# One decoder kernel, last attention: row sums from added pairs of exponential tiles, and the queries' copy on another engine

## The chip, the cores and the metric

The kernel runs on one core of a Trainium2 chip. A core has several engines with a queue of instructions each: TensorE (PE) for matmuls, VectorE (DVE) and ScalarE (ACT) for element-wise work, GpSimd (POOL), and SyncE (SP), which issues transfers here. Matmuls write to PSUM, and the other engines move results from there to SBUF. The metric is device microseconds of one execution.

## What is computed

A decoder of four blocks, each with self-attention, cross-attention to a context, and a feed-forward part. The change is in the last cross-attention. Batch 4, 256 queries of width 128, a context of 1601 rows of width 96, 16 heads of width 64:

```python
def _L3_xattn_ref(x, context, Wq, Wk, Wv, Wo, bo):
    HEADS, DIM_HEAD = 16, 64
    b, n, _ = x.shape
    h, d = (HEADS, DIM_HEAD)
    scale = d ** (-0.5)
    q = (x @ Wq).reshape(b, n, h, d).transpose(0, 2, 1, 3)
    k = (context @ Wk).reshape(b, -1, h, d).transpose(0, 2, 1, 3)
    v = (context @ Wv).reshape(b, -1, h, d).transpose(0, 2, 1, 3)
    sim = jnp.einsum('bhid,bhjd->bhij', q, k) * scale
    attn = jax.nn.softmax(sim, axis=-1)
    out = jnp.einsum('bhij,bhjd->bhid', attn, v)
    out = out.transpose(0, 2, 1, 3).reshape(b, n, h * d)
    return out @ Wo + bo
```

The softmax needs, for each query, the maximum of the scores over 1601 keys, the exponentials, their sum (the row sum, which the output is divided by), and their product with the values.

## The kernel before

The network runs in stages. `l3_xattn` is the last. It goes through 32 units: a batch and a pair of heads (`hp`) each. A unit has four steps of up to four chunks of 128 keys. Scores are held transposed, keys on the partitions: `scores(g)` makes a tile `St` of 128 x 1024 for two chunks (two heads x two chunks x 256 queries). Steps 0 to 2 have two such tiles (k = 0 to 5), step 3 has one of 65 rows (k = 6). Everything is float32.

The pieces of a unit, with the names by which the trace shows them:

- `queries` (L1894): projection of the queries by TensorE, copied from PSUM to the tile `Q` (L1900). `projections` (L1902): keys of one step and values of another, copied by ScalarE to `K` and `V` (L1931).
- `scores` (L1933): `big<-Q,K` on TensorE, copied by ScalarE to `St` (L1943).
- `running` (L1945): VectorE keeps the element-wise maximum of the unit's tiles in `kept[:, :4]` (shown as `w`; L1950 for the first two, L1953 for the others) and folds the two chunks (L1957).
- `maxima` (L1959): TensorE transposes the folded maxima (`one<-c,mx`), VectorE reduces (L1969). `spread` (L1971): TensorE brings the maxima back to all key rows (`one<-c,mq`), ScalarE copies them to `Mb` (L1981).
- `shifted` (L1983): VectorE subtracts `Mb` from each `St` in place (L1987). `weights` (L1991): ScalarE takes exponentials in place (L1994).
- `sums` (L1996): TensorE multiplies values and exponentials (`one<-St,V`), and then the exponentials by 32 columns of ones (`one<-St,c`), four products a tile: head h and chunk c go to their own strip of 32 partitions in the upper half of the accumulator `acc`. A float32 product is two records in the trace.
- `ended` (L2029): when a unit's sums are complete, ScalarE copies the strips to `rows` (L2026), TensorE adds them over chunks with the matrix `both`, VectorE takes the reciprocal (L2035) and multiplies (L2038). After a batch's eighth unit there follow the output projection (`one<-w,w`), the residual and normalisation (L535, L486 to L497) and, in `l3_ffn`, the quantised last layer (L2091 to L2122).

The order on TensorE, VectorE and ScalarE is written out by hand in the loop at L2061; each engine works its queue strictly in that order. Iteration `g` works on step `g` of the scores and, five steps later (`gb = g - LAG`), on the exponentials; the sums come one iteration after that. So in the iteration with `g % 4 == 0` stand the last running maximum of one unit, the shift of step 3 and the sums of step 2 of the unit before, and the maxima; in the next one the spread and the shift of step 0.

Small PSUM tiles (`misc`, shown as `one`) have two buffers; `acc`, the queries' projection, the maxima and the spread share them.

The stage starts while two chains of the stage before (batches 2 and 3 of the fourth self-attention layer, `life` at L1739 with `late` true) are still unfinished. They are carried over and advanced once an iteration (`later`). Their tiles `h`, `x1`, `x3` and `xn` lie in parts of the tile `kept`, which `places` hands out (L1885): `h` is `kept[:, 4:8]`.

Of the kernel before, what the change touches and what calls it, by code (L numbers as in the profile page):

```python
# [21 lines left out]
B, T, D = 4, 256, 128  # L22
# [281 lines left out]
class Net:  # L304
# [1416 lines left out]
    def l3_attn(self):  # L1721
        nc = self.nc
        slots = []
        for g in range(4):
            t = self.tile(f"QK{g}", [P, 2, T], bufs=1)
# [13 lines left out]
        def life(b):  # L1739
            if b == B - 1:  # L1740
                yield from self.taken_over()[0]
            start = x = self.x[b]
            for i in range(NL):
                pk = f"p3_{i}"
                late = i == NL - 1 and b >= B - 2
                if not late:
                    xb = self.tile("xb", wide, bufs=4)
                    nc.gpsimd.tensor_add(xb, x, row(pk, "bo"))
                if i or b not in self.ahead:
                    self.ahead[b] = yield from self.normed_T(  # L1750
                        x, self.w(pk, "ln1_w"), self.w(pk, "ln1_b")
                    )
                xT = self.ahead[b]
                values[b] = self.self_values(b, self.w(pk, "Wv"), self.w(pk, "bv"), xT, 8)
                ps = self.misc()
                self.mm(ps[:, :T], self.w(pk, "Wq"), xT)
                self.mm(ps[:, T:], self.w(pk, "Wk"), xT)
                qk = self.tile("qk", [P, 2, T], bufs=4)
                nc.scalar.activation(qk[:, 0, :], ps[:, :T], AF.Identity, bias=self.w(pk, "bq"))
                nc.vector.tensor_scalar_add(qk[:, 1, :], ps[:, T:], self.w(pk, "bk"))  # L1760
                outs[b] = self.tile("heads", wide, bufs=4, pool=self.act)
                ready[b], left[b] = (i, qk), 4
                yield
                while left[b]:
                    yield
                yield CUT if late else None
                if late:
                    xb = self.tile("xb", wide, bufs=1)
                    nc.gpsimd.tensor_add(xb, x, row(pk, "bo"))
                oT = self.transposed(  # L1770
                    outs[b], "oT", bufs=1 if late else 2, engine=nc.scalar
                )
                yield
                ps = self.misc()
                for n in range(NB):
                    self.mm(
                        ps[:, n * D : (n + 1) * D], oT[:, n * P : (n + 1) * P], self.w(pk, "Wo")
                    )
                x1 = self.late("x1") if late else self.tile("x1", wide, bufs=4)
                nc.vector.tensor_add(x1.rearrange(flat), ps[:, : NB * D], xb.rearrange(flat))  # L1780
                xb = self.tile("xb", wide, bufs=1 if late else 4)
                nc.gpsimd.tensor_add(xb, x1, row(pk, "b2"))
                xT = yield from self.normed_T(
                    x1, self.w(pk, "ln2_w"), self.w(pk, "ln2_b"), self.late("xn") if late else None
                )
                h = self.late("h") if late else self.tile("h", [P, 4, T])
                banks = {}
                for k in range(4):
                    if k % 2 == 0:
                        banks[k // 2] = self.misc()  # L1790
                    at = banks[k // 2][:, k % 2 * T : (k % 2 + 1) * T]
                    self.mm(at, self.w(pk, "W1")[:, k * P : (k + 1) * P], xT)
                    if k == 1 and not late:
                        continue
                    for j in ((k - 1, k) if late else range(4)) if k % 2 else ():
                        nc.scalar.activation(
                            h[:, j, :], banks[j // 2][:, j % 2 * T : (j % 2 + 1) * T], AF.Gelu,
                            bias=self.w(pk, "b1")[:, j : j + 1],
                        )
                yield  # L1800
                yield
                ps = self.misc()
                w2 = self.w(pk, "W2").rearrange("p (c d) -> p c d", c=4)
                for n in range(NB):
                    to = ps[:, n * D : (n + 1) * D]
                    for c in range(4):
                        self.mm(
                            to, h[:, c, n * P : (n + 1) * P], w2[:, c, :],
                            start=c == 0, stop=c == 3,
                        )  # L1810
                if late:
                    x = self.late("x3")
                elif i == NL - 2 and b >= B - 2:
                    x = self.y()
                else:
                    x = self.tile("x3", wide, bufs=4)
                nc.vector.tensor_add(x.rearrange(flat), ps[:, : NB * D], xb.rearrange(flat))
                finished[i] += 1
                if i == 0 and finished[0] == B:
                    self.load("p5")  # L1820
            z = yield from self.normed_steps(
                x, "xn", bufs=2, out=self.late("xn") if b >= B - 2 else None
            )
            nc.gpsimd.tensor_mul(z, z, row("p5", "fw"))
            nc.gpsimd.tensor_add(z, z, row("p5", "fb"))
            yield
            y = self.y()
            nc.vector.tensor_add(y, z, start)
            yield from self.block_end_steps(b, y)
# [35 lines left out]
    def l3_xattn(self):  # L1865
# [5 lines left out]
        nc = self.nc  # L1871
# [4 lines left out]
        steps = 4 * len(units)  # L1876
        qs, ks, vs, sts, mx, top, accs, outs = {}, {}, {}, {}, {}, {}, {}, {}
# [4 lines left out]
        nc.gpsimd.tensor_copy(wb, w8.bitcast(I8))  # L1882
        kept = self.tile(f"w{SLOT['p3_1']}", [P, 11, T], pool=self.wpool)
        one = [kept[:, i].rearrange("p (n d) -> p n d", n=NB) for i in range(8, 11)]
        places = {"h": kept[:, 4:8], "x1": one[0], "x3": one[1], "xn": one[2]}  # L1885
        self.late = places.get

        def parts(g):
# [5 lines left out]
        def queries(u):  # L1894
            b, hp = units[u]
            ps = self.misc()
            for d in halves:
                self.mm(ps[d, :T], wq[:, hp * P + d.start : hp * P + d.stop], self.xT[b])
            qs[u] = self.tile("Q", [P, T], bufs=2)
            nc.vector.tensor_copy(qs[u], ps[:, :T])  # L1900

        def projections(gk, gv):  # L1902

# [87 lines left out]
        def weights(g):  # L1991
            for k, nc_, kp in parts(g):
                e = sts[g // 4, k][:kp, :, :nc_, :]
                nc.scalar.activation(e, e, AF.Exp, scale=HD**-0.5)  # L1994

        def sums(g):  # L1996
            u = g // 4
            if g % 4 == 0:
                accs[u] = self.misc()
            acc = accs[u]  # L2000
            es = [(k, nc_, sts.pop((u, k))[:kp]) for k, nc_, kp in parts(g)]
            for k, nc_, e in es:
                for c in range(nc_):
                    i = 2 * k + c
                    for h, d in enumerate(halves):
                        if i < NCH - 1:
                            self.mm(
                                acc[d, :T], vs[g][:, i - g % 4 * 4, d], e[:, h, c, :],
                                start=i == 0, stop=False,
                            )  # L2010
            for k, nc_, e in es:
                kp = e.shape[0]
                for c in range(nc_):
                    for h in range(2):
                        d = slice(HD * h + SW * c, HD * h + SW * c + SW)
                        self.mm(
                            acc[d, T:], self.w("c", "ones", kp)[:, :SW], e[:, h, c, :],
                            start=False, stop=False,
                        )
                if kp < P:  # L2020
                    for h, d in enumerate(halves):
                        self.mm(acc[d, :T], vs[g][:kp, 0, d], e[:, h, 0, :], start=False)
            vs.pop(g)
            if g % 4 == 3:
                rows = self.tile("rows", [P, T], bufs=1)
                nc.scalar.copy(rows, acc[:, T:])  # L2026
                later.append(ended(u, rows))
# [32 lines left out]
        with self.tc.manual_schedule(engines=engines):  # L2060
            for g in range(-1, steps + LAG + 2):  # L2061
                gb = g - LAG
                if g % 4 < 2 and 0 <= g - 1 < steps:
                    running(g - 1)
                if g % 4 == 1 and 4 < g <= steps + 1:
                    spread(g // 4 - 1)
                if 0 <= gb < steps:
                    shifted(gb)
                if 0 <= g + 1 < steps and (g + 1) % 4 == 0:
# [11 lines left out]
                    running(g - 1)  # L2081
                if 0 <= g < steps:
                    scores(g)
            while later:
                self.advance(later)

# [58 lines left out]
```

## Time and profile before

| | us |
|---|---|
| three runs | 2769.0, 2773.4, 2780.3 (median 2773.41) |
| profiled execution, its own time | 2769.6 |
| its span, first to last instruction | 2767.8 |
| mean granted TensorE clock | 0.98 |
| last attention, from its first projection of queries | 1896.7 to the end |

Busy time from 1896.7 us to the end (871.1 us): TensorE 847.2, VectorE 610.5, ScalarE 552.3, GpSimd 23.3. Durations of single instructions in the stage (mean, taken from 2100 to 2750 us by shape):

| line, what | ns |
|---|---|
| L1987 shift, VectorE, 128x1024 | 1218 |
| L1953 running maximum, VectorE, 128x1024 | 1220 |
| L1950 first maximum, VectorE, 128x1024 | 1225 |
| L2035 reciprocal, VectorE, 128x256 | 1757 |
| L1900 queries' copy, VectorE, 128x256 | 416 |
| L1994 exponentials, ScalarE, 128x1024 | 1079 |
| L1943 score copy, ScalarE, 128x1024 | 1023 |
| L2026 copy of strips, ScalarE, 128x256 | 373 |

How to read it: a line of the timeline gives the start in us from the beginning of the span, the length, the engine, the line of the kernel, the operation with output<-input, the shape (partitions x elements), a count where like instructions follow each other, and in brackets the idle time before it with what ended that. Lengths of neighbours may overlap a little, since an engine begins an instruction before the one ahead has fully ended; the distance from start to start is what a queue needs. Several matmuls on different strips of the array run at once, so the mean of one record times the count is more than the time they take.

### The profile page before, as it was taken

What the parts mean: (1) busy time and instruction counts of PE and PEld (TensorE: products, weight loads), DVE (VectorE), ACT (ScalarE), POOL (GpSimd) and SP (SyncE); (2) the same over time, 40 slices, a digit from 0 to 9 for tenths busy, and PEclk for the clock granted to TensorE, in tenths of its full rate; (3) what the DMA queues carried; (4) which work ended last, traced back from release to release, by engine and by line L of the source; (5) the groups of instructions that cost most, each with busy time, mean ns of one, the idle gap of its engine ahead of it and who ended that gap; (6) DMA issues with size and microseconds to landing.
All of it is one profiled execution on the core that took longest, in us unless ns stands there. A gap on an engine that the chain in (4) does not pass through costs nothing.

```text
span 2767.8 us, 63295 instructions
## 1 busy us (share of the span) xinstructions
PE 2620.8 (95%) x26619; PEld 1708.1 (62%) x26619; DVE 1747.2 (63%) x3802; ACT 1526.2 (55%) x2931; POOL 180.2 (7%) x199
## 2 busy tenths in 40 slices
PE   6999999988879999999899999999999999999997
PEld 4555555555555555555797777776566666666665
DVE  5666666465457665655355666666677677677675
ACT  2455555635534555555554555556666576576573
POOL 2000100120020000000001011111000000000000
PEclk8999999989999999999999999999999999999999
DMA  3000000000120000000002010000000000000000
GB/s 111 2 1 1 2 1 1 1 21 15 27 88 17 2 1 1 1 2 1 1 1 87 20 25 13 13 12 3 1 1 2 4 2 1 3 2 2 3 2 3
DMA packets 14684, 34.57 MB, mean 12 GB/s; under 512 B 4025, under 2 KB 7229, under 8 KB 13505
## 3 DMA queue, kind: packets, MB, share of 16 engines
q1 hardware_dynamic: 14400, 30.53, 4.0%
q8 instruction: 210, 3.44, 0.5%
q14 instruction: 74, 0.60, 0.1%
HBM read 23.67 MB, written 0.52 MB: 9 GB/s over the span
## 4 chain that ended last, share of the span: by engine, by line
PE 88%; DVE 6%; ACT 3%; issue 2%; POOL 1%; DMA 0%; POOLq 0%; ACTq 0%; DVEq 0%
PE one L399 63%; PE big L399 13%; PE acc L399 8%; DVE M L909 1%; PE one L835 1%; PE one L544 1%; PE one L472 1%; DVE St L1987 1%; PE one L1324 1%; DVE mpad L697 1%; ACT E L731 0%; DVE w L1953 0%; DVE rec L2035 0%; POOL rn L1257 0%; ACT w L1314 0%
## 5 line engine op out<-in xcount | busy, mean ns | idle before, releaser
L909 DVE TENSOR_REDUCE M<-one 128x1 f32<-128x458 f32 (+3 forms) x1024 | 528.2, 567 | 290.8 <-PE one L399 289.8
L932 ACT ACTIVATE E<-one 128x512 f32<-128x512 f32 (+1 forms) x896 | 457.7, 563 | 420.8 <-PE one L399 420.7
L399 PE MATMUL one<-Q,K 32*128 32x256 f32 (+1 forms) x3328 | 531.8, 402 | 1.5 <-DVE M L909 1.5
L399 PE MATMUL one<-K,Q 32*128 32x458 f32 (+3 forms) x2048 | 459.2, 541 | 1.6 <-DVE M L909 1.6
L399 PEld LDWEIGHTS one<-Q,K 32*128 32x128 f32 (+1 forms) x3328 | 310.6, 180 | 62.3 <-DVE M L909 35.5
L1943 ACT COPY St<-big 128x1024 f32<-128x1024 f32 (+1 forms) x224 | 204.3, 959 | 160.0 <-PE big L399 160.0
L399 PEld LDWEIGHTS one<-K,Q 32*128 32x128 f32 x2048 | 171.2, 185 | 143.8 <-issue 79.3
L1987 DVE TENSOR_TENSOR St<-St,Mb 128x1024 f32<-128x1024 f32 (+1 forms) x224 | 245.2, 1141 | 1.8 <-ACT Mb L1981 1.8
L399 PE MATMUL acc<-E,V 128*32 128x256 f32 (+1 forms) x3328 | 233.2, 387 | 7.1 <-ACT E L932 7.1
L1994 ACT ACTIVATE St<-St 128x1024 f32<-128x1024 f32 (+1 forms) x224 | 215.1, 1014 | 25.4 <-DVE St L1987 25.3
L731 ACT ACTIVATE E<-one 128x384 f32<-128x384 f32 (+1 forms) x352 | 154.3, 525 | 115.0 <-PE one L399 114.8
L399 PE MATMUL big<-Q,K 64*128 64x256 f32 (+1 forms) x1664 | 214.4, 393 | 0.0
L399 PE MATMUL one<-St,V 128*64 128x256 f32 (+1 forms) x1664 | 205.7, 384 | 0.4
L492 POOL TENSOR_TENSOR ln_r<-ln_ve,half 128x2 f32<-128x2 f32 x92 | 71.0, 772 | 2070.0 <-DVE ln_ve L490 2015.8
L1953 DVE TENSOR_TENSOR w<-w,St 128x1024 f32<-128x1024 f32 (+1 forms) x160 | 178.5, 1116 | 34.8 <-ACT St L1943 27.6
L399 PE MATMUL one<-xT,w 128*128 128x256 f32 (+1 forms) x664 | 170.9, 398 | 18.8 <-DVE Q L1127 8.3
L692 DVE TENSOR_REDUCE Ms<-one 128x3 f32<-128x384 f32 x256 | 130.1, 550 | 89.0 <-PE one L399 87.8
L399 PEld LDWEIGHTS big<-Q,K 64*128 64x128 f32 (+1 forms) x1664 | 147.7, 183 | 57.5 <-issue 40.2
L399 PEld LDWEIGHTS acc<-E,V 128*32 128x32 f32 (+1 forms) x3328 | 87.3, 109 | 125.0 <-issue 70.0
L399 PEld LDWEIGHTS one<-St,V 128*64 128x64 f32 (+1 forms) x1664 | 114.3, 137 | 63.4 <-issue 15.9
L399 PEld LDWEIGHTS big<-w,ctx 96*64 96x64 f32 x1664 | 96.8, 137 | 54.0 <-issue 53.9
L399 PEld LDWEIGHTS one<-xT,w 128*128 128x128 f32 (+1 forms) x664 | 97.1, 181 | 50.2 <-issue 15.6
(308 smaller groups left out, 3743.7 us busy)
## 6 DMA issues: line engine op xcount, KB each, us to landing
QK<-qk SPq DMA_DIRECT2D x256, 16.0 KB
w<-in_p SPq DMA_DIRECT2D x12, 274.0 KB
rows<-in_ctx_rows SPq DMA_DIRECT2D x4, 630.5 KB
ctx<-in_ctx SPq DMA_DIRECT2D x4, 600.4 KB
w<-in_down SPq DMA_DIRECT2D x1, 2112.0 KB
w<-in_up SPq DMA_DIRECT2D x1, 1632.0 KB
w<-in_gp SPq DMA_DIRECT2D x1, 1632.0 KB
w<-in_p SPq DMA_DIRECT2D x4, 384.0 KB
```

Source lines behind the costliest of these rows:

```text
L399: self.nc.tensor.matmul(out, lhsT, rhs, start=start, stop=stop)
L472: self.nc.tensor.transpose(ps[:, n * P : (n + 1) * P], x[:, n, :], self.ident)
L492: nc.gpsimd.tensor_tensor(rstd, ve, self.half[:, :NB], ALU.pow)
L544: self.nc.tensor.transpose(ps[:rows, n * P : (n + 1) * P], m4[:, n, :rows], self.ident)
L692: nc.vector.reduce_max(out=m[:, j, :], in_=ps[:, : 3 * P].rearrange("p (s c) -> p s c", c=P), axis=AX.X,)
L731: nc.scalar.activation(es[t, j], ps[:, :w], AF.Exp, scale=scale)
L909: nc.vector.reduce_max(out=ms[i][:, n, j, part : part + 1], in_=ps[:, at : at + hi - lo], axis=AX.X)
L932: nc.scalar.activation(e[:kp, :w], ps[:kp, :w], AF.Exp, scale=scale)
L1943: nc.scalar.copy(st[:kp, :, :nc_, :], ps[:kp, :, :nc_, :])
L1953: nc.vector.tensor_max(to, to, sts[u, k][:kp, :, :nc_, :])
L1987: nc.vector.tensor_sub(e, e, top[u][:kp].unsqueeze(2).broadcast_to([kp, 2, nc_, T]))
L1994: nc.scalar.activation(e, e, AF.Exp, scale=HD**-0.5)
```

## The change

Three things are changed in the last attention.

1. A new function `added(g)` has VectorE add the two tiles of exponentials of a step into `kept[:, 4:8]`. It is called for step 2 of a unit in the iteration after its exponentials, behind `running` and ahead of `shifted`, and for step 0 at the end of the iteration that makes its exponentials. `sums` then multiplies only the sum by the ones: 4 products instead of 8.
2. A flag `busy` guards the buffer. The late chains wait for it and hold it from their entry until `x3` is made; `added` does nothing while it is held, and then the step's row sums are taken as before.
3. The queries' copy goes from VectorE to ScalarE.

```diff
@@ life(b)
                 yield CUT if late else None
+                while late and self.late("busy")[0]:
+                    yield
                 if late:
+                    self.late("busy")[0] = True
                     xb = self.tile("xb", wide, bufs=1)
...
                 nc.vector.tensor_add(x.rearrange(flat), ps[:, : NB * D], xb.rearrange(flat))
+                if late:
+                    self.late("busy")[0] = False
@@ l3_xattn
-        places = {"h": kept[:, 4:8], "x1": one[0], "x3": one[1], "xn": one[2]}
+        busy, pairs = [False], {}
+        places = {"busy": busy, "h": kept[:, 4:8], "x1": one[0], "x3": one[1], "xn": one[2]}
@@ queries(u)
-            nc.vector.tensor_copy(qs[u], ps[:, :T])
+            nc.scalar.copy(qs[u], ps[:, :T])
@@
+        def added(g):
+
+            if not busy[0]:
+                u, k = g // 4, g % 4 * 2
+                busy[0] = True
+                pairs[g] = kept[:, 4:8].rearrange("p (h c) t -> p h c t", h=2)
+                nc.vector.tensor_add(pairs[g], sts[u, k], sts[u, k + 1])
@@ sums(g)
-            for k, nc_, e in es:
+            if g in pairs:
+                busy[0] = False
+            for k, nc_, e in [(0, 2, pairs.pop(g))] if g in pairs else es:
                 kp = e.shape[0]
@@ loop over g
                 if g % 4 == 1 and 4 < g <= steps + 1:
                     spread(g // 4 - 1)
+                if gb % 4 == 3 and 0 < gb <= steps:
+                    added(gb - 1)
                 if 0 <= gb < steps:
                     shifted(gb)
...
                 if 0 <= g < steps:
                     scores(g)
+                if gb % 4 == 0 and 0 <= gb < steps:
+                    added(gb)
```

## The prediction

> **What bounds the kernel now.** The page first: TensorE (PE) is busy for 95% of the span and makes up 88% of the chain that ended last.
>
> ```profile
> PE 2620.8 (95%) x26619; PEld 1708.1 (62%) x26619; DVE 1747.2 (63%) x3802; ACT 1526.2 (55%) x2931; POOL 180.2 (7%) x199
> ...
> PE 88%; DVE 6%; ACT 3%; issue 2%; POOL 1%; DMA 0%; POOLq 0%; ACTq 0%; DVEq 0%
> ```
>
> A busy PE is not a PE at its peak, so I go to the stage. The last attention runs from about 1897 us to the end: 32 units (a pair of heads of one batch), each of four steps, of which 19 follow each other at 24.59 us (from one row of L1969 to the next). The busy time of the engines in one such unit (columns: window, length, busy PE, PEld, DVE, ACT, POOL, granted clock, DMA share, GB/s):
>
> ```profile
> 2211.99:2236.58 24.59, 24.59 (x268) 15.43 (x264) 17.93 (x18) 16.86 (x24) 0.00 (x0) 1.00 0.01 1
> ```
>
> PE has no gap; VectorE (DVE) is idle for 6.66 us. Last the timeline of that unit, which shows what waits for what (start, length, engine, line, output<-input, count, idle time before it):
>
> ```profile
> 2210.99 1.07 PE L399 MATMUL one<-St,c 128*32 128x256 f32 x16
> 2212.00 1.09 PE L399 MATMUL one<-c,mx 128*64 128x128 f32 x16
> ...
> 2217.36 4.62 DVE L1987 TENSOR_TENSOR St<-St,Mb 128x1024 f32<-128x1024 f32 x4
> 2217.70 0.62 PE L399 MATMUL one<-St,c 65*32 65x256 f32 x4
> ...
> 2218.26 0.65 PE L399 MATMUL one<-St,V 65*64 65x256 f32 x4
> 2218.36 0.59 ACT L1931 COPY V<-big 128x512 f32<-128x512 f32 x1
> 2218.84 2.02 ACT L1994 ACTIVATE St<-St 128x1024 f32<-128x1024 f32 x2
> ...
> 2222.53 1.76 DVE L2035 RECIPROCAL rec<-one 128x256 f32<-128x256 f32 x1 [0.55 <-PE one L399]
> ...
> 2224.66 2.54 DVE L1953 TENSOR_TENSOR w<-w,St 128x1024 f32<-128x1024 f32 x2
> ```
>
> ```profile
> 2229.73 2.54 DVE L1953 TENSOR_TENSOR w<-w,St 128x1024 f32<-128x1024 f32 x2
> ...
> 2232.05 0.65 PE L399 MATMUL big<-Q,K 64*65 64x256 f32 x4
> ...
> 2233.41 0.69 DVE L1953 TENSOR_TENSOR w<-w,St 65x512 f32<-65x512 f32 x1 [1.14 <-ACT St L1943]
> ...
> 2234.14 0.69 DVE L1957 TENSOR_TENSOR mx<-w 128x512 f32<-128x512 f32 x1
> ...
> 2234.75 0.68 DVE L1987 TENSOR_TENSOR St<-St,Mb 65x512 f32<-65x512 f32 x1
> ...
> 2235.58 1.07 PE L399 MATMUL one<-St,c 128*32 128x256 f32 x16
> ```
>
> Call T0 the start of the ones-matmuls of step 2 (2210.99, next 2235.58). The reader is to see two places: the four shifts of 2217.36 run without a gap although the exponentials of the first two end only at 2220.86; and between the small scores (2232.05) and T0 VectorE has only running maximum, fold and one small shift.
>
> **The change part by part.**
>
> *PE, removed.* Step 0 and step 2 keep 8 of 16 records of one<-St,c. Sixteen take 1.00 us from start to start (2206.46 to 2207.46; here to 2212.00); a group of 4 records, which on two column strips runs in two turns as 8 will on four, takes 0.56 (2217.70 to 2218.26). So an add removes 0.44 us, 0.88 in a full unit. The flag leaves the additions out while the late chains of batches 2 and 3 hold the buffer: unit 0 has one, units 2 and 3 none, all others two, 59 in all. 59 x 0.44 = 26 us if nothing else moved.
>
> *VectorE, added.* An add is a tensor_tensor of 128x1024 like L1950: 1.22 us, 1.14 to the next independent instruction (2216.22 to 2217.36 there). Its place on the queue decides.
>
> Add of step 0: it stands between the shifts of steps 0 and 1 and waits for both exponentials of step 0. These end at T0 + 9.87 now (2220.86), and T0 + 9.43 with the shorter ones-matmuls. The shifts of step 0 are over at about T0 + 8.2, so VectorE stands still for 1.2 us, and all that is queued behind waits with it: shifts of step 1, reciprocal, product, maxima of step 1, shifts and maxima of step 2, maximum of step 3, fold, and the second add.
>
> Add of step 2: it stands behind the fold, ahead of the small shift, and the ones-matmuls of step 2 wait for it. From the start of the small scores PE comes to them 3.53 us later (2232.05 to 2235.58); the fold lets an add start after 2.70 (2234.75), so it ends at 3.92 and PE can start at 3.97, with the 0.05 that PE takes after VectorE (the maxima's reduce ends at 2724.97, PE starts at 2725.02). Even with VectorE on time PE waits 0.44, as much as this add saves it.
>
> The loop from T0 to T0, all from rows of this unit: first add starts T0 + 9.46 (0.03 after ScalarE, as at L1953: copy ends 2233.38, maximum 2233.41); + 1.14 add; + 2.27 two shifts (2227.12 to 2229.39); + 1.79 reciprocal; + 0.34 product; + 2.46 maxima of step 1 (2224.66 to 2227.12); + 2.27 shifts of step 2; + 2.64 maxima of step 2 (each is followed by one that needs its result, 1.32 as in the row of three at 2182.44); + 0.73 and 0.61 maximum of step 3 and fold; + 1.22 second add; + 0.05 = 24.98. That is 0.39 more than 24.59: **VectorE's queue with the wait in it becomes the bound**, and PE, which would need 23.71, idles about 1.27 a unit, most of it ahead of the ones-matmuls of step 2.
>
> *Queries' copy.* 0.42 (0.34 to the next) leaves VectorE; the loop above has it out already. ScalarE takes 0.37 for such a copy (L2026). It comes behind the score copies of step 2, where ScalarE idled 1.20 before K<-big, so it is hidden; without that cover it would cost 0.37 at most. In a batch's last unit PE waited 0.48 for the copy by VectorE; that goes. The queries' matmul needs the buffer which the product frees, at T0 + 15.1 in the new order, and PE is there at T0 + 15.1: nothing lost.
>
> *Units beside the regular 19.* (a) Three times a batch ends. In the unit with the output projection (2145.34 to 2154.33) VectorE idles 9.15 us and catches up, so PE decides: - 0.88 - 0.48 + 0.44 = -0.9. In the next one VectorE has 2.37 us of output chain behind the first add (2172.36 to 2174.73), 0.51 further on (2181.93 to 2182.44), and the quantisation before the maxima's reduce, which makes PE's spread 0.31 later: 24.98 + 2.37 + 0.51 + 0.31 = 28.2 against 25.67 (2160.74 to 2186.41), +2.5. Together +1.6, three times +4.8. (b) Units 0 to 4: -0.44 up to unit 3, then unit 4, with 1.27 (as at 1924.58 to 1925.85) + 0.51 of late layernorm in the loop and no shortened ones-matmul at its start (+ 0.44): 27.2 against 25.11, +2.1; together +1.7. (c) The last interval has little PE work (22.44); the loop makes it 25.0, +2.5; in the tail behind it some 0.9 is gained.
>
> Sum: 19 x 0.39 = 7.4, + 4.8 + 1.7 + 2.5 - 0.9 = **+15.5 us**.
>
> **Two rules against the rows.** The Trainium skill (Perfetto Trace Analysis, Identifying the Most-Contended Engine) calls occupancy a fair measure for VectorE and says to work on the engine with most of it. VectorE would have 17.93 - 0.41 + 2.44 = 19.96 us in a unit, 84% of PE's 23.71; by that rule PE stays the bound and all 26 us are won. The timeline says +15.5, since VectorE's 1.2 us of waiting and the 9.46 before the first add are in the loop. I take the timeline.
>
> The second concerns the new PE waits. The skill (TensorE: Matmul & The Clock Gate, What's actually happening) has the clock halve after an idle window of about 3.4 us; waits of 1.3 would be free. This trace halves it sooner: after 1.54 us of idling, with 0.80 a little before, the granted clock is 0.50 (columns as above):
>
> ```profile
> 2729.00:2730.00 1.00, 0.00 (x1) 0.00 (x0) 1.00 (x2) 0.92 (x2) 0.00 (x0) 1.00 0.00 0
> ...
> 2732.00:2733.00 1.00, 1.00 (x8) 0.63 (x6) 1.00 (x1) 0.88 (x1) 0.00 (x0) 0.50 0.00 0
> ```
>
> There sixteen matmuls with V took 3.46 instead of 1.90 us. But single waits of 1.03 to 1.10 us amid dense matmuls (thirteen between 82 and 1229 us) left it at 1.00, and so did 1.25 at 1523; only one of 1.16 at 616.7, in a stretch with other gaps, was followed by 0.51. Sparse stretches are not this stage, so the forecast has no halving; its price by the row of 3.46 would be 1.6 us each time.
>
> **The rivals.**
>
> 1. *The additions are hidden.* If VectorE's idle 6.66 us took them in and PE stayed the bound: -26 us, **2744**. For it: occupancy, and PE's full timeline. Against it: the order of VectorE's queue, above. It needs the loop under 23.71, 1.3 us less than its rows give; if only the step 2 add showed, half would be left, -13, 2757. Chance 0.11.
>
> 2. *The clock halves at the new waits.* Place: the 1.27 us before the ones-matmuls of step 2, with maxima, scores and spread right behind them in the loop. Price 1.6 us a unit; in half of some 28 units +22, **2807**, in all +45, 2830. From about 1.5 us of idling in one stretch it decides. For it: the rows above and a wait of some 2 us after each batch's end, where the output chain holds a PSUM buffer. Against it: the single short waits. Chance 0.18.
>
> 3. That the change doesn't do what it says is out: the changed program has the 59 additions on VectorE.
>
> **How the numbers follow.** The profiled execution took 2769.6 us (span 2767.8, 1.8 around it); +15.5 gives 2785.1. The median of the three runs is 2773.4, 3.8 above it, which would give 2788.9; I take **2787**. Forecast 0.71, within it about +7 to +23 (0.2 us a unit either way, and the batch ends). Half a percent, about what a measurement of this kernel can tell from no change, is 13.9 us; the forecast lies just above, so a good half of it counts as slower, and rival 2 with it: slower 0.56, same 0.33, faster 0.11. The range, 2764 to 2815, takes in the forecast, the near half of rival 2 and a little of the step toward rival 1.
>
> **What would show it.** L1969 to L1969 in regular units at 25.0, not 23.7 or 24.6; the first add with about 1.2 us idle ahead of it, released by the exponentials; PE idle 1.2 us at one<-w,c of step 2, released by the add; granted clock in the stage near 1.00. A regular period of 24.2 or less would show that the first add's wait is taken in; half a clock after the waits, rival 2.

## The result and the profile after

The changed kernel takes 2791.12 us (median; 2787.7 to 2792.14) against 2774.3 us for the kernel before (2769.01 to 2780.34): a ratio of **1.0061, with the 95% interval from 1.0047 to 1.0076**. The forecast was 2787 us, slower. The profiled execution took 2792.14 us.

The page of the changed kernel, its busy time by engine and the chain that ended last:

```profile
PE 2608.4 (93%) x26147; PEld 1707.5 (61%) x26147; DVE 1804.7 (65%) x3829; ACT 1540.0 (55%) x2963; POOL 178.9 (6%) x199
...
PE 72%; DVE 18%; ACT 6%; issue 3%; POOL 1%; DMA 0%; DVEq 0%; SPq 0%; ACTq 0%; POOLq 0%
```

PE has 472 records fewer (26619 to 26147, 59 additions of eight), and its share of the chain went from 88% to 72%. VectorE has it instead: 6% to 18%. The windows view of one regular unit, from one reduce of the maxima (now L1975) to the next (window, length, busy PE, PEld, DVE, ACT, POOL, granted clock, DMA share, GB/s):

```profile
2222.82:2247.80 24.98, 23.86 (x250) 15.25 (x252) 19.88 (x20) 17.35 (x25) 0.00 (x0) 1.00 0.00 1
```

The unit was 24.59 us long with PE at work throughout. Now it is 24.98, and PE works 23.86 of it. VectorE, at 19.88 of 24.98 (80%), looks far from full. Yet the timeline of this unit shows that its queue sets the length (start, length, engine, line, output<-input, count, idle time before it and its releaser):

```profile
2228.51 2.02 ACT L2000 ACTIVATE St<-St 128x1024 f32<-128x1024 f32 x2
...
2230.56 1.23 DVE L2008 TENSOR_TENSOR w<-St,St 128x1024 f32<-128x1024 f32 x1 [1.17 <-ACT St L2000]
...
2231.70 2.35 DVE L1993 TENSOR_TENSOR St<-St,Mb 128x1024 f32<-128x1024 f32 x2
...
2240.83 3.35 DVE L1959 TENSOR_TENSOR w<-w,St 128x1024 f32<-128x1024 f32 x3
...
2244.21 0.69 DVE L1963 TENSOR_TENSOR mx<-w 128x512 f32<-128x512 f32 x1
...
2244.82 1.22 DVE L2008 TENSOR_TENSOR w<-St,St 128x1024 f32<-128x1024 f32 x1
...
2246.09 0.64 PE L399 MATMUL one<-w,c 128*32 128x256 f32 x8 [1.11 <-DVE w L2008]
...
2255.54 1.22 DVE L2008 TENSOR_TENSOR w<-St,St 128x1024 f32<-128x1024 f32 x1 [1.17 <-ACT St L2000]
```

Read it from the top. ScalarE ends the exponentials at 2230.53, VectorE's first addition has waited 1.17 us for them, and the shifts of the next step stand behind it. From there VectorE does not stop: reciprocal, product, maxima, shifts, maxima, fold, second addition. PE waits 1.11 us for that one, and its ones-matmuls start the next unit, in which the exponentials end and the first addition starts 9.45 us later (2255.54). That closes the loop. Neither engine is full in it: PE waits once for VectorE, and VectorE once for exponentials that ScalarE can only make behind PE's earlier matmuls. In PE's waits over the whole stage (engine and tile, what is waited for: us in all, times, longest) the addition of step 2 is the largest row:

```profile
PE one L399 <- DVE w L2008: 30.9, 30, 2.9
...
PE one L399 <- DVE y L2134: 5.4, 3, 1.8
```

**Where the time came from**, from the first reduce of the maxima to the end of both profiled runs:

| part of the stage | before, us | after, us | difference |
|---|---|---|---|
| 19 regular units | 24.59 each | 18 at 24.98, one 25.33 | +7.8 |
| three batch ends (two units each) | 34.44 + 25.50 | 34.49 + 27.38, 34.50 + 26.81, 34.49 + 26.80 | +4.7 |
| units 0 to 4 | 140.00 | 140.10 | +0.1 |
| last interval | 22.44 | 26.04 | +3.6 |
| behind the last reduce | 43.52 | 44.18 | +0.7 |

The sum is +16.9; the medians differ by 16.8. The two profiled spans differ by 22.6. The other 5.7 us lie ahead of the first reduce: 1.2 of them before the stage, and the rest where TensorE's clock was granted at 0.50 for the first 9 us of the stage, but at 1.00 in the profile before. In the runs below that first reduce came anywhere between 1907 and 1925 us with no relation to the edits, and the same half clock stands there in two of them, so I count this as chance. The unit of 25.33 us, the first regular one behind a batch end, ran at a clock of 1.00 throughout; VectorE paused there for about 0.4 us between two running maxima, for no reason that the trace shows.

### The profile page after: what moved, and what is told of

Same layout as the page of the kernel before. It is cut to its first block, busy times and chain, and to the rows that moved or that the text cites. A ratio compares the mean times of both kernels' runs of the same rounds, so it can differ in the third digit from the quotient of the medians.

```text
span 2790.4 us, 62380 instructions
## 1 busy us (share of the span) xinstructions
PE 2608.4 (93%) x26147; PEld 1707.5 (61%) x26147; DVE 1804.7 (65%) x3829; ACT 1540.0 (55%) x2963; POOL 178.9 (6%) x199
## 4 chain that ended last, share of the span: by engine, by line
PE 72%; DVE 18%; ACT 6%; issue 3%; POOL 1%; DMA 0%; DVEq 0%; SPq 0%; ACTq 0%; POOLq 0%
PE one L399 54%; PE acc L399 8%; PE big L399 6%; DVE w L1959 5%; DVE St L1993 3%; DVE w L2008 2%; ACT St L2000 2%; DVE rec L2051 2%; DVE M L909 1%; PE one L835 1%; PE one L544 1%; DVE mx L1963 1%; PE one L472 1%; ACT K L1937 1%; PE one L1324 1%
```

## The experiments

All edits are made to the changed kernel, but for one. "Period" is the length of a regular unit, as above. Each ratio is to runs of the kernel before that were made together with it: their median is 2772.67 us for parts 1 and 2, and 2771.36 us for parts 3 and 4. A difference between two medians of different parts is therefore good to a few us only.

**1. Each addition alone.** The first run leaves out the call for step 2:

```
                     spread(g // 4 - 1)
-                if gb % 4 == 3 and 0 < gb <= steps:
-                    added(gb - 1)
```

> Only the addition of step 0 is left (same place on VectorE, so with its wait for the exponentials); step 2 takes its row sums from both tiles as before. Loop theory: without the second addition nothing of VectorE stands ahead of the ones-matmuls of step 2, and the fold is ready at T0 + 24.2 where the maxima need it at T0 + 25.2, so TensorE decides again: regular period 24.59 - 0.44 = 24.15, time about 13 us under before (2761, ratio 0.995). Rival, that the wait at the first addition alone costs what was seen: period stays near 25. Rival, occupancy alone: also 24.15, but then the second addition would have brought as much again.

Measured: 2764.34 us, ratio 0.9975 (0.9958 to 0.9993), period 24.24. The second run leaves out the call for step 0:

```
                     scores(g)
-                if gb % 4 == 0 and 0 <= gb < steps:
-                    added(gb)
```

> Only the addition of step 2 is left, at its place behind the fold. Loop theory: it saves 0.44 us of ones-matmuls and TensorE waits 0.44 for it, so the regular period is 24.59 again and the time within 0.1% of before (a microsecond or two less through the queries' copy). TensorE idles about 0.4 us ahead of the ones-matmuls of step 2, released by the addition. Rival, occupancy: period 24.15, 12 us less.

Measured: 2769.01 us, ratio 0.9991 (0.9972 to 1.0011), period 24.59. The timeline with the addition of step 0 alone:

```profile
2216.32 1.23 DVE L2008 TENSOR_TENSOR w<-St,St 128x1024 f32<-128x1024 f32 x1 [1.17 <-ACT St L2000]
```

The same 1.17 us of waiting, but no other addition behind it, and the whole is a gain. It is some 8 us and not the 13 expected: the period misses by 0.09 us, and the batch ends gain nothing (33.36 + 26.75 us against 34.44 + 25.50). The timeline with the addition of step 2 alone:

```profile
2215.05 0.64 PE L399 MATMUL one<-w,c 128*32 128x256 f32 x8 [0.37 <-DVE w L2008]
```

Here PE waits 0.37 us and saves 0.44 by having eight records fewer, and the period stays at 24.59: what the addition saves, the wait for it takes back. So neither addition costs time by itself. Together they do: the second comes later by the first one's wait. The 0.09 us by which the first period missed its 24.15 is nearly all in a gap of 0.08 ahead of the queries' matmul (it starts 2.01 us behind the scores ahead of it, and 1.93 where VectorE's product comes earlier). That PE waits there for the PSUM buffer that the product frees is my reading; no row names it.

**2. The same additions elsewhere.** If the first addition's wait is the cause, it must go when the addition stands behind the next step's shifts, where its input has long been ready:

```
                 if 0 <= gb < steps:
                     shifted(gb)
+                if gb % 4 == 1 and 0 <= gb < steps:
+                    added(gb - 1)
...
-                if gb % 4 == 0 and 0 <= gb < steps:
-                    added(gb)
```

> Both additions, the same work, but the one of step 0 stands behind the shifts of step 1 instead of ahead of them; its exponentials end at T0 + 9.4 and it starts at T0 + 10.5, so it waits for nothing. Loop theory: VectorE's chain ends at T0 + 23.7, the second addition waits for the small scores (T0 + 20.18 + 3.97), period 24.15, time about 12 us under before (2762). If the work of the additions and not the wait were the cause, the period stays at 24.98 and the time at 2791.

Measured: 2763.1 us, ratio 0.9967 (0.9952 to 0.9983), period 24.16. Then the addition of step 2 is also moved, from behind the last running maximum and the fold to ahead of that maximum:

```
                 gb = g - LAG
+                if gb % 4 == 3 and 0 < gb <= steps:
+                    added(gb - 1)
                 if g % 4 < 2 and 0 <= g - 1 < steps:
                     running(g - 1)
...
-                if gb % 4 == 3 and 0 < gb <= steps:
-                    added(gb - 1)
```

> As e3, and the addition of step 2 stands ahead of the last running maximum, in the 1.14 us in which VectorE waited for the copy of the small scores. Loop theory: neither addition is waited for, TensorE decides: period 24.59 - 0.88 = 23.71, time about 25 us under before (2749, ratio 0.991), faster than both kernels. If VectorE's work is the cause, no better than e3; if the addition there delays the fold past the maxima, a period between 23.7 and 24.2.

Measured: **2749.49 us, ratio 0.9916 (0.9891 to 0.9941)**, period 23.72. The timeline of the first of the two:

```profile
2232.53 4.62 DVE L1993 TENSOR_TENSOR St<-St,Mb 128x1024 f32<-128x1024 f32 x4
2237.07 1.22 DVE L2008 TENSOR_TENSOR w<-St,St 128x1024 f32<-128x1024 f32 x1
```

Four shifts run without a gap again, as before the change, and the addition follows without waiting. The timeline of the second, with both moved:

```profile
2223.76 1.22 DVE L2008 TENSOR_TENSOR w<-St,St 128x1024 f32<-128x1024 f32 x1
...
2224.90 0.68 DVE L1959 TENSOR_TENSOR w<-w,St 65x512 f32<-65x512 f32 x1
...
2226.56 0.64 PE L399 MATMUL one<-w,c 128*32 128x256 f32 x8
```

The second addition now fills a gap: the running maximum has to wait anyway until ScalarE has copied its scores out. It ends about 1.6 us before PE needs it, where PE had waited. The unit in the windows view (columns as above):

```profile
2204.55:2228.27 23.72, 23.72 (x250) 14.91 (x252) 19.70 (x20) 17.13 (x25) 0.00 (x0) 1.00 0.01 1
```

PE is full once more. VectorE works as much as in the changed kernel (19.70 against 19.88 us) and PE does as many matmuls (250); only the places on VectorE's queue differ. They are worth 24.98 - 23.72 = 1.26 us a unit, 39.1 us in the two profiles from the first reduce to the end, and 41.6 us between the medians of the two kernels. This version beats both.

**3. The queries' copy.** Once back on VectorE, and once alone: the kernel before with nothing but that line.

```
             qs[u] = self.tile("Q", [P, T], bufs=2)
-            nc.scalar.copy(qs[u], ps[:, :T])
+            nc.vector.tensor_copy(qs[u], ps[:, :T])
```

> The changed kernel with the queries' copy back on VectorE. Loop theory: the copy stands in VectorE's loop between the shifts and the maxima of step 2 and lengthens every regular unit by its 0.34 us: period 25.32 instead of 24.98, time about 8 us over the changed kernel (2799, ratio to before about 1.009). If VectorE's queue were not the bound of the changed kernel, the copy would be hidden and the period 24.98.

Measured: 2807.74 us, ratio 1.0127 (1.0103 to 1.0152), period 25.31. The period is as expected: 0.33 of the copy's 0.42 us comes through, so VectorE's queue holds the loop. The total is some 9 us more than expected. What the loop does not explain lies in the units with the output projection, 38.91, 38.90 and 37.33 us instead of 34.5, and in the second interval of the stage, 29.03 instead of 24.97, where PE waited 2.59 us for the same copy. In three of these four a half clock followed (last section), which is the difference from 37.33 to 38.91. The timeline of the first output projection:

```profile
2152.97 0.41 DVE L1906 COPY Q<-one 128x256 f32<-128x256 f32 x1
...
2153.44 2.77 PE L399 MATMUL one<-w,w 128*64 128x128 f32 x16 [2.58 <-DVE Q L1906]
```

PE's output projection needs the buffer that this copy empties, and the copy stands behind VectorE's late shifts. The change to ScalarE hides more than I had priced: with the additions it is worth 2807.74 - 2791.12 = 16.6 us between the medians (20.4 in the two profiles from the first reduce to the end). The line alone:

> The kernel before with only the queries' copy on ScalarE, no additions. TensorE decides: period 24.59, the unit with the output projection 0.48 us shorter, three times, since TensorE no longer waits there for VectorE's copy. Time 1 to 2 us under before, not to be told from it. A period away from 24.59 would mean that ScalarE's queue matters.

Measured: 2769.42 us, ratio 0.9993 (0.9977 to 1.0009), period 24.59. Without additions PE's full unit hides the copy on either engine. Only the unit with the output projection gets clearly shorter each time, by 0.70 (34.44 to 33.74), 2 us in three. The 0.48 expected was the wait as the row shows it; from start to start, the projection stood 1.53 us behind the matmuls ahead of it, and now stands 0.87.

**4. A third addition.** By the busy time alone VectorE still has 4 us free in the best version's unit. So the addition of step 1 was put to it, ahead of the shifts of step 2:

```
+                if gb % 4 == 2 and 0 <= gb < steps:
+                    added(gb - 1)
                 if 0 <= gb < steps:
                     shifted(gb)
```

> As e4, with a third addition, of step 1, behind its maxima and ahead of the shifts of step 2. TensorE alone would need 24.59 - 1.32 = 23.27. Loop theory: VectorE has another 1.14 us in the way from the unit's first maximum to the fold; the fold then ends at T0 + 24.7 and the maxima's matmuls stand 0.57 behind the next T0, so the period is about 24.1: slower than e4 by 0.4 us a unit, though VectorE would be busy for only 21.0 us of it. By occupancy it would be faster than e4 (23.3 a unit, some 12 us).

Measured: 2768.98 us, ratio 0.9986 (0.9972 to 1.0001), period 24.18: 0.46 longer than with two, although the third addition takes eight more matmul records off PE in each unit. The timeline:

```profile
2220.85 1.09 PE L399 MATMUL one<-c,mx 128*64 128x128 f32 x16 [0.78 <-DVE mx L1963]
```

Now it is the fold of the maxima that comes too late, and PE waits for it in 26 units (19.2 us in all).

## Why the prediction was right

**The loop.** Worked out as 24.98 from start-to-start times of single rows of the kernel before, measured as 24.98. The first addition was forecast 9.46 us after the ones-matmuls of step 2 with 1.2 us of idling ahead of it: measured 2255.54 - 2246.09 = 9.45, and 1.17. PE was to idle 1.2 us at the second addition: 1.11. Taking away either addition, or the first one's wait alone, shortens the period as the sum says it should, so the cause is shown, and not only its size.

**The 0.44 us of an addition**, priced from a group of four records on two column strips, holds: with the places changed the period falls by 0.43 and 0.44.

**Occupancy.** The rule of the Trainium skill (Perfetto Trace Analysis, Identifying the Most-Contended Engine), that the engine with the highest occupancy is to be worked on first, promised 26 us here when PE's busy time is taken as its occupancy (for PE the page itself calls that a poor measure of how close a kernel is to the peak). The runs decide against it twice: VectorE at 80% sets the period of the changed kernel, and the third addition takes work from the engine at 100% and lengthens the period by 0.46 us (19.5 us between the medians). Rival 1, 2744 us, fails for the reason that was given, the order of the queue. Its size was nearly right for another order: with both additions moved the kernel takes 2749.49.

**Rival 2, the halved clock,** did not occur where it was placed: all regular units kept 1.00. It occurred at rarer, longer waits. In the windows view of the changed kernel, two batch ends, each with the 1.80 us wait for the output chain (the row of y above):

```profile
2178.00:2181.00 3.00, 1.20 (x14) 0.47 (x12) 2.97 (x6) 3.00 (x6) 0.00 (x0) 0.93 0.00 0
2181.00:2184.00 3.00, 3.00 (x16) 1.54 (x16) 2.90 (x8) 0.61 (x1) 0.70 (x1) 0.50 0.02 5
2392.00:2394.00 2.00, 1.03 (x10) 0.74 (x12) 1.90 (x6) 1.74 (x2) 0.00 (x0) 1.00 0.00 0
2394.00:2397.00 3.00, 3.00 (x32) 1.93 (x30) 2.93 (x8) 0.34 (x1) 0.69 (x1) 1.00 0.00 0
```

After the first, 16 matmuls fill 3 us; after the second, 32. PE lost 1.53 us in the row with V (3.48 instead of 1.95), close to the 1.6 priced, but only 0.57 of it reached the unit (27.38 against 26.81). The timeline shows where the rest went: PE's wait for the second addition, 1.32 us in the undisturbed unit, was down to 0.36 in the other.

```profile
2195.77 0.64 PE L399 MATMUL one<-w,c 128*32 128x256 f32 x8 [0.36 <-DVE w L2008]
...
2407.32 0.64 PE L399 MATMUL one<-w,c 128*32 128x256 f32 x8 [1.32 <-DVE w L2008]
```

The prediction's case against rival 2 also overlooked a row. Of the single waits of 1.03 to 1.10 us in the kernel before, the one that ends at 1045.88 was followed by a half clock two us later; that it was the cause is not shown. The windows view there:

```profile
1047.84:1050.84 3.00, 3.00 (x28) 1.07 (x20) 1.40 (x3) 1.08 (x2) 0.00 (x0) 0.55 0.00 0
```

So a single wait of this length is no proof against a half clock, though none followed the 52 waits of 1.10 to 1.67 us that the last section counts.

**Terms of the sum:**
- *Batch ends, +4.8:* +4.7. By the reduces the split looks wrong, -0.9 and +2.5 forecast, +0.05 and +1.3 in the table. But the reduce at the end of the unit with the output projection now stands behind the quantisation on VectorE, 2.43 us after PE's transposes instead of 1.31, which moves time from the second unit to the first. From one start of those transposes (`one<-c,mx`) to the next, the unit with the projection went from 34.27 to 33.20 us (-1.1), and the one behind it from 25.67 to 28.10 (+2.4). The timeline:

```profile
2167.68 1.09 PE L399 MATMUL one<-c,mx 128*64 128x128 f32 x16
...
2169.90 0.29 DVE L2121 TENSOR_SCALAR q<-q 128x256 f32<-128x256 f32 x1
...
2170.11 0.68 DVE L1975 TENSOR_REDUCE mq<-one 128x4 f32<-128x512 f32 x1
```

- *Units 0 to 4, +1.7:* +0.1, the largest miss. Unit 4 lost 2.3, as forecast (2.1), but two of the units ahead of it gained 1.2 each, where 0.44 in all was put. One of these gains (37.82 to 36.67) needs no additions to explain it: the mean granted clock of that unit was 0.86 before and 0.91 after, and the run of the queries' copy alone, also at 0.91, has 36.35.
- *Last interval, +2.5:* +3.6. By the transposes it is +2.7 (22.43 to 25.16), as forecast; PE waited 2.94 us for the addition, and then the clock halved, which put off the reduce.
- *Tail, -0.9:* +0.7. Both profiles have a half clock in the tail, the one before at the row of 3.46 us, the one after right behind the last reduce, so this difference says little. Without that half clock the run of the copy alone has a tail of 41.88 us, 1.6 less than before.

The timeline of the last interval after the change:

```profile
2743.45 0.82 PE L399 MATMUL one<-w,c 128*32 128x256 f32 x8 [2.94 <-DVE w L2008]
2744.20 1.98 PE L399 MATMUL one<-c,mx 128*64 128x128 f32 x16
```

The sixteen matmuls of the second row take 1.98 us; in a regular unit they take 1.09.

## What to carry to other kernels

- An engine with idle time takes more work for nothing only at a place on its queue where the input is ready already, or where the queue stands still anyway. The same two additions gave 1.0061 at one pair of places and 0.9916 at another.
- To price an instruction on an in-order queue, follow the loop from one start to the same start a unit later, with every wait in it, and compare its length with the time that the fullest engine needs; in these runs the longer of the two was the period.
- Moving a copy to another engine may be worth nothing alone (0.9993) and 16.6 us beside another edit, so test edits together as well as alone.
- Before reading a split between neighbouring units, check that the instruction that marks their border has not itself moved: here VectorE's reduce had, by 1.1 us, and PE's transposes had not.

## What the runs showed of the hardware

The clock halved after shorter waits of PE than the ~3.4 us idle window that the Trainium skill gives (TensorE: Matmul & The Clock Gate, What's actually happening), and not after every wait of the same length. In the changed kernel it halved after none of the regular waits of 1.11 us, after one of three of 1.80, and after the one of 2.94. Over the nine profiles, from the first reduce on:

| PE's wait, us | a granted clock of 0.50 in the 3 us behind it |
|---|---|
| 1.10 to 1.67, amid dense matmuls | 0 of 52 |
| 1.54, in the last units, where other waits are near | 5 of 8 |
| 1.80 | 4 of 9 |
| 1.90 to 2.07 | 1 of 7 |
| 2.58 and 2.59 | 3 of 4 |
| 2.94 | 1 of 2 |
| 4.22 and more | 18 of 18 |

With the queries' copy back on VectorE, PE waited 2.58 us at each of the three output projections; the windows view of that run, just behind each (columns as above):

```profile
2155.00:2157.00 2.00, 2.00 (x9) 1.34 (x8) 0.00 (x0) 0.00 (x0) 0.00 (x0) 0.50 0.00 0
2374.00:2376.00 2.00, 2.00 (x9) 1.54 (x9) 0.00 (x0) 0.00 (x0) 0.00 (x0) 0.50 0.00 0
2592.00:2594.00 2.00, 2.00 (x19) 1.75 (x17) 0.00 (x0) 0.00 (x0) 0.00 (x0) 1.00 0.00 0
```

Two halved and the third did not, with the same matmuls at the same point of the loop; these are the units of 38.91, 38.90 and 37.33 us. Below 3.4 us the length of the wait does not decide it alone: waits of about 2 us halved the clock less often than waits of 1.54. The same section says that the window is free-running, and that the point of the transition depends on where in it a kernel's first matmul falls; outcomes that differ at the same place would fit that, but no run here shows it. PE busy at a half clock reads as full: only the count (9 against 19 records in 2 us) and the clock column tell it.
